# A selective scan on one core: C's rows kept in SBUF, the entering state multiplied in on ScalarE, one more product on GpSimd

## The chip, the core and the metric

The kernel runs on one core of a Trainium2 chip. The metric is device time in microseconds of one execution of the whole program, the median of several runs. Durations of single instructions come from one profiled execution.

## The reference

The input is a float32 image batch of 2 x 96 channels x 128 x 128. Two layers follow each other; each adds a token mixer and then a small quantised feed-forward net. The feed-forward nets and the second layer's mixer (a 3 x 3 convolution) are not touched here. The first layer's mixer is four Mamba scans over the image, in four directions (rows forward, rows backward, columns forward, columns backward), each with 192 inner channels d and 16 states s, over L = 16384 tokens:

```python
def step(h, t):
    dt_t, u_t, B_t, C_t = t
    dA = jnp.exp(dt_t[:, :, None] * A)
    h = dA * h + dt_t[:, :, None] * B_t[:, None, :] * u_t[:, :, None]
    y = jnp.einsum('bds,bs->bd', h, C_t)
    return (h, y)
...
y = ys.transpose(1, 0, 2) + Dp * xc
y = y * jax.nn.silu(z)
return y @ outp_w.T
```

B and C depend on token and state, not on the channel: every one of the 192 channels of a direction is multiplied with the same row. The four results are concatenated and mixed by a 96-row matrix (fuse_w).

## The kernel before

For each of the two images there are three stages: `normalize` (layer norm, and a copy of the image by columns), `mamba` (all scans), and `ffn_and_conv`. The change lies in `mamba` and in the layout of its weights.

**Tiling.** Directions are handled in two pairs (rows forward with columns forward, then the two backward ones). A pair has 2 x 192 = 384 channels, that is NG = 3 groups of 128 partitions: group 0 is the first 128 channels of the first direction, group 2 the last 128 of the second, and the middle group 1 holds 64 channels of each. Tokens are cut in tiles of T = 512. A **step** is one pair and one tile of tokens: 2 x 32 = 64 steps an image. A **unit** is one group and two states: 24 units a step. Two units, so four states, make a **quad**, the piece in which rows of B and C are loaded: [128 partitions, 4 states, 512 tokens], 1 MB.

**Rows of B and C.** For each step a matrix product gives the rows of B and C of both directions (`rows`, L262 to L272), and one DMA writes them to the DRAM tile `bcd` (L277), laid out [B or C, quad of states, direction, state, token]. `row_tile` (L329) loads a quad back, repeated over the partitions. For groups 0 and 2 one direction's rows go to all 128 partitions. For group 1 both directions are needed, and the source is stated as 64 repeats of the pair of directions, so that even partitions get the first direction and odd ones the second:

```python
src = d["bcd"][k, s // 4] if g == 1 else d["bcd"][k, s // 4, g // 2 : g // 2 + 1]
n = src.shape[0]
nc.sync.dma_start(t, src[None].broadcast_to((128 // n, n, 4, T)))
```

So that the channels stand in the same order, the weights of group 1 are permuted on the host (`perm` in `_layout`), and where group 1 comes out of a product in halves, it is written to a tile `mix` first and then moved by two DMAs to even and odd partitions (`mix`, L253 to L256).

**A unit.** GpSimd multiplies a quad of B in place by dt * u (`b_part`, L339). ScalarE writes the two decays exp(dt * A) of a unit into PSUM (`decay`, L349). VectorE scans the two states over 512 tokens (L353); the result goes over the decays in PSUM. VectorE multiplies it by C (L441), into C's tile. TensorE adds the products of all 16 states into one PSUM bank `y` by products with the identity (`sums`, L357). For the six units of `BY_POOL`, (g, s) with s 0 or 8, the scan's result goes to SBUF into B's tile, and GpSimd makes the product with C (L360), since only SBUF is open to it in this kernel. ScalarE keeps each scan's last column in `hst` (L442).

**How a step takes over the state.** Scans start from 0.0. For a step after the first, ScalarE computes the first token's decay for all 16 states of a group (`entry`, L303), GpSimd multiplies it by `hst` (L342) and adds it to the first token of each quad of B (L343).

**Order.** Instructions go to each engine in the order in which the program issues them (`manual_schedule`). The main loop (L469 to L490) runs over units k. At even k it fetches the B quad of unit k + 6 (`B_AHEAD` = 3 quads) and lets GpSimd work on the quad of unit k + 2, then come the scan of the first state, the product and the sums of unit k - 1 (`behind`), the decays of unit k + 2, the scan of the second state, and at even k the fetch of C's quad of unit k + 4 (`C_AHEAD` = 2). `later` puts GpSimd's products one iteration after and their sums three iterations after. The next step's projections, convolutions and activations (`prologue`) are issued between units at fixed places in the previous step. All loads of the stage but two go through SP's queue. `row0` has four buffers and `row1` three; a fetch waits on SP for the sums, products or scans that read the buffer last.

Of the kernel before, what the change touches and what calls it, by code (L numbers as in the profile page):

```python
# [10 lines left out]
F32 = mybir.dt.float32  # L11
# [3 lines left out]
AF = mybir.ActivationFunctionType  # L15
# [16 lines left out]
NG = 3  # L32
B_AHEAD = 3
C_AHEAD = 2
AHEAD = 2
BY_POOL = tuple((g, s) for g in range(3) for s in (0, 8))
BCO = 32
# [4 lines left out]
def tile_metaformer(ctx: ExitStack, tc: tile.TileContext, a: dict, out: bass.AP):  # L42
# [142 lines left out]
    def mamba(acc, xnr, xnc):  # L185

        with ExitStack() as st:
            pool = lambda n, bufs, **kw: st.enter_context(tc.tile_pool(name=n, bufs=bufs, **kw))

            io, gen, one, mixp, two = (pool(*p) for p in (("io", 2), ("gen", 4), ("one", 1), ("mixp", 1), ("two", 2)))  # L190
            ps_w, ps_y, ps_m = (pool(n, k, space=PSUM) for n, k in (("ps_w", 3), ("ps_y", 1), ("ps_m", 1)))
            rows_d = pool("rows_d", 3, space=DRAM)

            hst = one.tile([128, NG, S], F32, name="hst")
            enter = one.tile([128, NG, S], F32, name="enter")
            acc_w = acc.rearrange("c (h w) -> c w h", w=W)
# [17 lines left out]
            def prologue(pi, i, d):  # L214
# [20 lines left out]
                def conv_out(g):  # L235
                    if g == 1:
                        d["xc"] = two.tile([128, NG, T], F32, name="xc")
                    t = mixed("xc") if g == 1 else d["xc"][:, g, :]
                    nc.scalar.activation(t, d["ps"], AF.Identity, bias=convb[:, pi, g : g + 1])  # L239

# [3 lines left out]
                def gate_out(g):  # L244
                    if g == 1:
                        d["sz"] = two.tile([128, NG, T], F32, name="sz")
                    nc.scalar.copy(mixed("sz") if g == 1 else d["sz"][:, g, :], d["ps"])  # L247

                def mixed(name):
                    d["mix", name] = mixp.tile([128, T], F32, name="mix")  # L250
                    return d["mix", name]

                def mix(name):  # L253

                    for k in range(2):
                        nc.sync.dma_start(d[name][k:128:2, 1, :], d["mix", name][64 * k : 64 * k + 64, :])  # L256

# [42 lines left out]

                def entry(g):

                    nc.scalar.activation(enter[:, g, :], amat[:, pi, g, :], AF.Exp, scale=d["dt"][:, g, 0:1])  # L303

                first = pi == 0 and i == 0
                at = [(-3, 1, load), (3, 0, partial(mix, "xc")), (11, 0, partial(silu, "xc"))]
                at += [(9, 0, partial(mix, "sz")), (31, 1, partial(silu, "sz"))]
                at += [(12, 0, rows), (13, 1, rows_out), (14, 0, rows_to_dram)]  # L310
# [9 lines left out]
                for g, k in enumerate((19, 27, 29)):  # L320
                    at += [(k, 0, partial(dt_u, g))]
                    if i > 0:
                        at += [((20, 24, 29)[g], 1, partial(entry, g))]

# [3 lines left out]

            def row_tile(d, g, s, k, ahead):  # L329

                t = gen.tile([128, 4, T], F32, name=f"row{k}", bufs=ahead + 1)

                src = d["bcd"][k, s // 4] if g == 1 else d["bcd"][k, s // 4, g // 2 : g // 2 + 1]
                n = src.shape[0]
                nc.sync.dma_start(t, src[None].broadcast_to((128 // n, n, 4, T)))
                return t

            def b_part(i, d, g, s, b):
                nc.gpsimd.tensor_tensor(b, d["dtu"][g][:, None, :].broadcast_to((128, 4, T)), b, ALU.mult)  # L339
                if i > 0:  # L340
                    if s == 0:
                        nc.gpsimd.tensor_tensor(enter[:, g, :], enter[:, g, :], hst[:, g, :], ALU.mult)  # L342
                    nc.gpsimd.tensor_tensor(b[:, :, 0], b[:, :, 0], enter[:, g, s : s + 4], ALU.add)  # L343

            def decay(pi, d, g, s):

                da = ps_w.tile([128, 2, T], F32, name="da")
                for j in range(2):
                    nc.scalar.activation(da[:, j, :], d["dt"][:, g, :], AF.Exp, scale=amat[:, pi, g, s + j : s + j + 1])  # L349
                return da  # L350

            def scan(j, da, b, h):
                nc.vector.tensor_tensor_scan(h[:, j, :], da[:, j, :], b[:, j, :], 0.0, ALU.mult, ALU.add)  # L353

# [4 lines left out]
            def by_pool(h, c):  # L359
                nc.gpsimd.tensor_tensor(c, h, c, ALU.mult)  # L360

# [52 lines left out]

            def fetch(k, n, ahead, m):
                if k < total:
                    t = row_tile(state[k // nu], *units[k % nu], n, ahead)
                    m[k], m[k + 1] = t[:, 0:2, :], t[:, 2:4, :]
                    if n == 0:
                        quads[k] = t  # L420

            def feed(k):

                if k < total:
                    n = k // nu
                    b_part(steps[n][1], state[n], *units[k % nu], quads.pop(k))

            def feed_decay(k):
                if k < total:
                    n = k // nu  # L430
                    das[k] = decay(steps[n][0], state[n], *units[k % nu])

            ys = {}

            def behind(k):

                n, u = divmod(k, nu)
                (pi, i), d, (g, s) = steps[n], state[n], units[u]
                h, c = hs.pop(k), cs.pop(k)
                if (g, s) not in BY_POOL:  # L440
                    nc.vector.tensor_tensor(c, h, c, ALU.mult)  # L441
                nc.scalar.copy(hst[:, g, s : s + 2], h[:, :, T - 1])  # L442
                if s == 0:
                    if k > 0:
                        pn, pu = divmod(k - 1, nu)
                        gated(steps[pn][0], state[pn], units[pu][0], ys.pop(k - 1))
                    y = ps_y.tile([128, T], F32, name="y")
                    nc.tensor.matmul(y, dmat[:, pi, g, :], d["xc"][:, g, :], start=True, stop=False)  # L448
                else:
                    y = ys.pop(k - 1)  # L450
                ys[k] = y
                if (g, s) in BY_POOL:
                    later(k + 1, 1, True, by_pool, h, c)
                    later(k + 3, 1, True, sums, s, y, c)
                else:
                    sums(s, y, c)
                if k == total - 1:
                    gated(pi, d, g, y)
                if s == S - 2 and g > 0:
                    later(k + 4, 0, True, project, pi, i, d, g)  # L460
                    later(k + 5, 1, False, collect, pi, d, g)

            for m, (n, ahead) in ((bs, (0, B_AHEAD)), (cs, (1, C_AHEAD))):
                for k in range(ahead):
                    fetch(2 * k, n, ahead, m)
            feed(0)
            for k in range(AHEAD):
                feed_decay(k)
            for k in range(total + 6):  # L469
                n, u = divmod(k, nu)  # L470
                if u == nu - 3:

                    prepare(n + 2)
                if k % 2 == 0:
                    fetch(k + 2 * B_AHEAD, 0, B_AHEAD, bs)
                    feed(k + AHEAD)
                issue(k, 0)
                if k < total:
                    (g, s) = units[u]
                    da, b = das.pop(k), bs.pop(k)  # L480
                    hs[k] = b if (g, s) in BY_POOL else da
                    scan(0, da, b, hs[k])
                if 0 < k <= total:
                    behind(k - 1)
                feed_decay(k + AHEAD)
                if k < total:
                    scan(1, da, b, hs[k])
                if k % 2 == 0:
                    fetch(k + 2 * C_AHEAD, 1, C_AHEAD, cs)
                issue(k, 1)  # L490
# [109 lines left out]
def _layout(v):  # L600
# [3 lines left out]

    perm = np.arange(2 * DI)
    perm[128:256] = perm[128:256].reshape(2, 64).T.reshape(-1)
    grouped = lambda w: w.reshape(2, NG, 128, -1).transpose(2, 0, 1, 3)
    plain = lambda w: grouped(w[order].reshape(2, 2 * DI, -1))
    rows = lambda w: grouped(w[order].reshape(2, 2 * DI, -1)[:, perm])
    xw = v["L0_conv_xproj_w"]  # L610
# [12 lines left out]
    for pi, (p, q) in enumerate(PAIRS):  # L623
        ow = v["L0_conv_outp_w"]
        outx[:, pi, 0] = ow[p, :, :128]
        outx[:, pi, 1, 0::2] = ow[p, :, 128:]
        outx[:, pi, 2, 1::2] = ow[q, :, :64]
        outx[:, pi, 3] = ow[q, :, 64:]
# [6 lines left out]
        "convb": plain(v["L0_conv_conv_b"])[..., 0],  # L635
        "bcw": grouped(bcw[:, perm]),
        "dtw": dtw[:, :, perm],
        "dtb": rows(v["L0_conv_dt_b"])[..., 0],
        "alog": rows(v["L0_conv_A_log"]),
        "dskip": rows(v["L0_conv_Dp"])[..., 0],  # L640
        "outx": outx,
# [27 lines left out]
```

## Time and profile before

| What | Value |
|---|---|
| Median of three runs | 11,550.38 us (11,546.19 to 11,551.36) |
| Profiled execution: time | 11,556.77 us |
| Profiled execution: span in the trace | 11,555.0 us |
| Granted TensorE clock, mean | 0.989 |
| HBM read / written | 3289.04 MB / 54.53 MB |
| Packets on SP's DMA queue | 539,960, 3410.16 MB, 76.8% of 16 engines over the span |

The time is that of the whole execution; the span runs from the first to the last recorded instruction. Engines are named PE (TensorE), PEld (its weight loads), DVE (VectorE), ACT (ScalarE), POOL (GpSimd) and SP (SyncE). A row of a group gives line, engine, operation, output and inputs, the count, the busy time, the mean duration of one in ns, and the engine's idle time just before these instructions with what ended it. Idle time of an engine that is not the bound costs nothing by itself.

### The profile page before, as it was taken

Reading aid. Unit: us, or ns where it says so; the run is one execution under the profiler, and the core shown is the slowest. Engines: PE = TensorE matmul, PEld = TensorE weight load, DVE = VectorE, ACT = ScalarE, POOL = GpSimd, SP = SyncE. Lnnn points to the kernel's source line nnn. Section 1 sums busy time; section 2 is a strip of 40 time slices with the busy share of each in tenths; the row PEclk is TensorE's granted clock in tenths of the full one; section 3 lists DMA queues with packets and bytes.
Section 4 is the critical chain, followed back from the end, with each engine's and each line's share of the span. In section 5 each row is a group of like instructions: output and inputs, shape, how many; then the busy total and the mean of one; then the engine's idle time right before and its main releaser. Section 6 shows DMA issues by size and latency. Waiting matters only on the chain. (4 is left out here: it accounts for less than half of the span.)

```text
span 11555.0 us, 94102 instructions
## 1 busy us (share of the span) xinstructions
PE 10435.0 (90%) x24208; PEld 3971.4 (34%) x24208; DVE 10421.6 (90%) x10127; ACT 7901.7 (68%) x13564; POOL 9672.3 (84%) x4700
## 2 busy tenths in 40 slices
PE   7999999999999999989989999999999999999899
PEld 2333333333333333333323333333333333333333
DVE  6999999999999999994469999999999999999944
ACT  6767767677677677665567677677676776776655
POOL 5999999999999999991159999999999999999911
PEclk8999999999999999999989999999999999999999
DMA  7888888888888888880068888888888888888800
GB/s 263 335 329 333 333 332 332 330 331 333 329 332 333 330 331 333 329 322 19 26 243 334 328 331 334 330 333 333 333 331 329 332 332 329 331 333 329 319 13 13
DMA packets 540755, 3416.96 MB, mean 296 GB/s; under 512 B 67532, under 2 KB 68652, under 8 KB 143832
## 3 DMA queue, kind: packets, MB, share of 16 engines
q1 hardware_dynamic: 539960, 3410.16, 76.8%
q8 instruction: 196, 3.21, 0.1%
q14 instruction: 343, 2.81, 0.1%
q0 software_dynamic: 256, 0.79, 0.0%
HBM read 3289.04 MB, written 54.53 MB: 289 GB/s over the span
## 5 line engine op out<-in xcount | busy, mean ns | idle before, releaser
L339 POOL TENSOR_TENSOR row<-dtu,row 128x2048 f32<-128x2048 f32 x1536 | 6948.9, 4524 | 283.3 <-DMA row<-bcd 281.6
L357 PE MATMUL y<-row,ident 128*128 128x512 f32 x12288 | 5690.6, 603 | 700.0 <-DVE row L441 699.9
L353 DVE TENSOR_TENSOR_SCAN da<-da,row 128x512 f32<-128x512 f32 x4608 | 5456.9, 1214 | 38.9 <-ACT da L349 5.2
L349 ACT ACTIVATE da<-dt,amat 128x512 f32<-128x512 f32 x6144 | 4246.9, 691 | 170.2
L357 PEld LDWEIGHTS y<-row,ident 128*128 128x128 f32 x12288 | 2256.8, 190 | 4008.4 <-issue 2243.5
L441 DVE TENSOR_TENSOR row<-da,row 128x1024 f32<-128x1024 f32 x2304 | 2776.7, 1205 | 70.2 <-DMA row<-bcd 70.0
L442 ACT COPY hst<-da 128x2 f32<-128x2 f32 x2304 | 368.9, 160 | 2652.2 <-DVE row L441 2649.3
L360 POOL TENSOR_TENSOR row<-row,row 128x1024 f32<-128x1024 f32 x768 | 1807.4, 2353 | 223.0 <-DVE row L353 147.5
L353 DVE TENSOR_TENSOR_SCAN row<-da,row 128x512 f32<-128x512 f32 x1536 | 1852.4, 1206 | 91.9 <-POOL row L339 84.1
L211 PE MATMUL misc<-xa,inx 96*64 96x512 f32 (+1 forms) x2048 | 946.1, 605 | 50.0 <-ACT mix L239 26.8
L211 PE MATMUL misc<-xb,inx 96*64 96x512 f32 (+1 forms) x2048 | 952.3, 608 | 33.6 <-ACT hst L442 24.2
L564 POOL TENSOR_TENSOR acc<-acc,y 96x512 f32<-96x512 f32 x128 | 147.4, 1151 | 991.5 <-DVE y L563 991.5
L298 POOL TENSOR_TENSOR dtu<-dt,xc 128x512 f32<-128x512 f32 x384 | 487.4, 1269 | 106.0 <-DMA xb<-xnc 99.8
L576 PE MATMUL pc<-pad,kw 96*96 96x512 f32 x1152 | 566.4, 593 | 0.0
L211 PEld LDWEIGHTS misc<-xa,inx 96*64 96x64 f32 (+1 forms) x2048 | 327.3, 165 | 581.2 <-issue 438.0
L448 PE MATMUL y<-xc,dmat 128*128 128x512 f32 x768 | 419.5, 628 | 103.6 <-DVE sz L364 103.6
L374 PE MATMUL misc<-sz,gmat 128*96 128x512 f32 x1024 | 484.1, 595 | 0.0
L284 PE MATMUL misc<-rows,dtw 12*128 12x512 f32 x768 | 434.3, 645 | 50.6 <-ACT dt L289 37.9
L364 DVE TENSOR_TENSOR sz<-y,sz 128x512 f32<-128x512 f32 x384 | 264.6, 689 | 229.5 <-PE y L357 198.0
L136 DVE TENSOR_TENSOR xq<-xm,rs 96x512 fp8e5<-96x512 f32 x128 | 87.9, 687 | 392.2 <-ACT rs L132 392.2
L211 PEld LDWEIGHTS misc<-xb,inx 96*64 96x64 f32 (+1 forms) x2048 | 316.5, 164 | 361.9 <-issue 214.1
L372 PE MATMUL misc<-acc,ident 96*96 96x512 f32 x512 | 387.6, 842 | 57.3 <-ACT sz L247 53.8
(76 smaller groups left out, 7449.9 us busy)
## 6 DMA issues: line engine op xcount, KB each, us to landing
row<-bcd SPq DMA_DIRECT2D x3072, 1024.0 KB, 7.4
xc<-mix SPq DMA_DIRECT2D x256, 128.0 KB, 5.4
sz<-mix SPq DMA_DIRECT2D x256, 128.0 KB, 8.9
xa<-xnr SPq DMA_DIRECT2D x124, 193.1 KB, 8.6
xb<-xnc SPq DMA_DIRECT2D x124, 193.1 KB, 8.7
bcd<-rows SPq DMA_DIRECT2D x128, 128.0 KB, 9.5
acc<-in_x_dram SPq DMA_DIRECT2D x16, 768.0 KB, 5.7
xnr<-xn SPq DMA_DIRECT2D x16, 768.0 KB, 4.3
```

The lines of the kernel that those rows point to most:

```text
L211: nc.tensor.matmul(ps[rows, :], w(PAIRS[pi][d], k, lo, hi), src[d][:, k : k + T], **se)
L284: nc.tensor.matmul(d["ps"], w, d["rows"][0 : 2 * RK, :], start=True, stop=True)
L298: nc.gpsimd.tensor_tensor(dtu, d["dt"][:, g, :], d["xc"][:, g, :], ALU.mult)
L339: nc.gpsimd.tensor_tensor(b, d["dtu"][g][:, None, :].broadcast_to((128, 4, T)), b, ALU.mult)
L349: nc.scalar.activation(da[:, j, :], d["dt"][:, g, :], AF.Exp, scale=amat[:, pi, g, s + j : s + j + 1])
L353: nc.vector.tensor_tensor_scan(h[:, j, :], da[:, j, :], b[:, j, :], 0.0, ALU.mult, ALU.add)
L357: nc.tensor.matmul(y, ident, c[:, j, :], start=False, stop=s + j == S - 1)
L360: nc.gpsimd.tensor_tensor(c, h, c, ALU.mult)
L374: nc.tensor.matmul(d["po"], gmat[:, pi, 2 * g - 2 + k, :], d["yg"][g - 1 + k], start=False, stop=k == 1)
L441: nc.vector.tensor_tensor(c, h, c, ALU.mult)
L448: nc.tensor.matmul(y, dmat[:, pi, g, :], d["xc"][:, g, :], start=True, stop=False)
L576: nc.tensor.matmul(pc, kw[:, t, :], rows, start=t == 0, stop=t == 8)
```

## The change

- C no longer streams. Four tiles `crow` [128, 4, 512], one for each quad of states, are kept. `c_fill` loads all 128 partitions of one for group 0, and then only the half whose direction changes: partitions 64 to 127 for group 1, partitions 0 to 63 for group 2. A fill is issued two quads after the units that read the tile last.
- The product with C is written into B's tile instead of C's.
- B has five buffers and is fetched four quads ahead, after the second scan of an iteration. Its source is now stated as each direction's rows repeated 64 times, one direction after the other, so that group 1 is two halves and not interleaved. `perm`, `mix` and the `mix` tile go.
- The state enters otherwise: ScalarE multiplies the first token's decay in PSUM by `hst`, one column per state, and the scan starts from 1.0 instead of 0.0. `entry`, the tile `enter` and GpSimd's additions go.
- GpSimd makes the products of seven units of 24: s = 2 and 8 of each group, and s = 4 of group 1.
- The scratch memory for DMAs that GpSimd issues is set to 4096 bytes.

```diff
-B_AHEAD = 3
-C_AHEAD = 2
+B_AHEAD = 4
-BY_POOL = tuple((g, s) for g in range(3) for s in (0, 8))
+BY_POOL = tuple((g, s) for g in range(3) for s in (2, 8)) + ((1, 4),)
...
-            def row_tile(d, g, s, k, ahead):
-
-                t = gen.tile([128, 4, T], F32, name=f"row{k}", bufs=ahead + 1)
-
-                src = d["bcd"][k, s // 4] if g == 1 else d["bcd"][k, s // 4, g // 2 : g // 2 + 1]
+            def row_tile(d, g, s):
+
+                t = gen.tile([128, 4, T], F32, name="row", bufs=B_AHEAD + 1)
+                src = d["bcd"][0, s // 4] if g == 1 else d["bcd"][0, s // 4, g // 2 : g // 2 + 1]
                 n = src.shape[0]
-                nc.sync.dma_start(t, src[None].broadcast_to((128 // n, n, 4, T)))
+                nc.sync.dma_start(t, src[:, None].broadcast_to((n, 128 // n, 4, T)))
                 return t
 
+            crow = [one.tile([128, 4, T], F32, name=f"crow{q}") for q in range(S // 4)]
+
+            def c_fill(n, g, q):
+
+                if n < len(steps):
+                    part = (slice(0, 128), slice(64, 128), slice(0, 64))[g]
+                    src = state[n]["bcd"][1, q, int(g > 0)]
+                    nc.sync.dma_start(crow[q][part], src[None].broadcast_to((part.stop - part.start, 4, T)))
+
-            def b_part(i, d, g, s, b):
+            def b_part(d, g, b):
                 nc.gpsimd.tensor_tensor(b, d["dtu"][g][:, None, :].broadcast_to((128, 4, T)), b, ALU.mult)
-                if i > 0:
-                    if s == 0:
-                        nc.gpsimd.tensor_tensor(enter[:, g, :], enter[:, g, :], hst[:, g, :], ALU.mult)
-                    nc.gpsimd.tensor_tensor(b[:, :, 0], b[:, :, 0], enter[:, g, s : s + 4], ALU.add)
...
+                if i > 0:
+                    for j in range(2):
+                        nc.scalar.activation(da[:, j, 0:1], da[:, j, 0:1], AF.Copy, scale=hst[:, g, s + j : s + j + 1])
                 return da
 
-            def scan(j, da, b, h):
-                nc.vector.tensor_tensor_scan(h[:, j, :], da[:, j, :], b[:, j, :], 0.0, ALU.mult, ALU.add)
+            def scan(i, j, da, b, h):
+                nc.vector.tensor_tensor_scan(h[:, j, :], da[:, j, :], b[:, j, :], float(i > 0), ALU.mult, ALU.add)
...
-                h, c = hs.pop(k), cs.pop(k)
+                h, b, c = hs.pop(k), cs.pop(k), crow[s // 4][:, s % 4 : s % 4 + 2, :]
                 if (g, s) not in BY_POOL:
-                    nc.vector.tensor_tensor(c, h, c, ALU.mult)
+                    nc.vector.tensor_tensor(b, h, c, ALU.mult)
...
                 if k % 2 == 0:
-                    fetch(k + 2 * C_AHEAD, 1, C_AHEAD, cs)
+                    fetch(k + 2 * B_AHEAD)
+                    if 4 <= k < total + 4:
+                        cn, cu = divmod(k - 4, nu)
+                        cg, cq = cu // 8, cu % 8 // 2
+                        c_fill(cn + (cg == 2), (cg + 1) % 3, cq)
                 issue(k, 1)
```

More of the change, by code (lines that the diff above doesn't have):

```diff
@@ L188, in mamba @@
             pool = lambda n, bufs, **kw: st.enter_context(tc.tile_pool(name=n, bufs=bufs, **kw))
-            io, gen, one, mixp, two = (pool(*p) for p in (("io", 2), ("gen", 4), ("one", 1), ("mixp", 1), ("two", 2)))
+            io, gen, one, two = (pool(*p) for p in (("io", 2), ("gen", 4), ("one", 1), ("two", 2)))
             ps_w, ps_y, ps_m = (pool(n, k, space=PSUM) for n, k in (("ps_w", 3), ("ps_y", 1), ("ps_m", 1)))
@@ L194, in mamba @@
             hst = one.tile([128, NG, S], F32, name="hst")
-            enter = one.tile([128, NG, S], F32, name="enter")
             acc_w = acc.rearrange("c (h w) -> c w h", w=W)
@@ L237, in conv_out @@
                         d["xc"] = two.tile([128, NG, T], F32, name="xc")
-                    t = mixed("xc") if g == 1 else d["xc"][:, g, :]
-                    nc.scalar.activation(t, d["ps"], AF.Identity, bias=convb[:, pi, g : g + 1])
+                    nc.scalar.activation(d["xc"][:, g, :], d["ps"], AF.Identity, bias=convb[:, pi, g : g + 1])
                 def gate(g):
@@ L246, in gate_out @@
                         d["sz"] = two.tile([128, NG, T], F32, name="sz")
[L247 to L256, printed above, removed]
+                    nc.scalar.copy(d["sz"][:, g, :], d["ps"])
                 def silu(name):
@@ L299, in dt_u @@
                     d["dtu"].append(dtu)
-                def entry(g):
-                    nc.scalar.activation(enter[:, g, :], amat[:, pi, g, :], AF.Exp, scale=d["dt"][:, g, 0:1])
                 first = pi == 0 and i == 0
-                at = [(-3, 1, load), (3, 0, partial(mix, "xc")), (11, 0, partial(silu, "xc"))]
-                at += [(9, 0, partial(mix, "sz")), (31, 1, partial(silu, "sz"))]
+                at = [(-3, 1, load), (11, 0, partial(silu, "xc"))]
+                at += [(31, 1, partial(silu, "sz"))]
                 at += [(12, 0, rows), (13, 1, rows_out), (14, 0, rows_to_dram)]
@@ L321, in prologue @@
                     at += [(k, 0, partial(dt_u, g))]
-                    if i > 0:
-                        at += [((20, 24, 29)[g], 1, partial(entry, g))]
                 outs = (conv_out, gate_out, rows_out, dt_out)
@@ L327, in prologue, with decay @@
                 return sorted(at, key=lambda p: p[:3])
[L329 to L333 removed]
+            def row_tile(d, g, s):
+                t = gen.tile([128, 4, T], F32, name="row", bufs=B_AHEAD + 1)
+                src = d["bcd"][0, s // 4] if g == 1 else d["bcd"][0, s // 4, g // 2 : g // 2 + 1]
                 n = src.shape[0]
[L335 removed]
+                nc.sync.dma_start(t, src[:, None].broadcast_to((n, 128 // n, 4, T)))
                 return t
[L338 to L345 removed]
+            crow = [one.tile([128, 4, T], F32, name=f"crow{q}") for q in range(S // 4)]
[5 more added lines that the diff above has]
+            def b_part(d, g, b):
+                nc.gpsimd.tensor_tensor(b, d["dtu"][g][:, None, :].broadcast_to((128, 4, T)), b, ALU.mult)
+            def decay(pi, i, d, g, s):
                 da = ps_w.tile([128, 2, T], F32, name="da")
@@ L359, in by_pool @@
             def by_pool(h, c):
-                nc.gpsimd.tensor_tensor(c, h, c, ALU.mult)
+                nc.gpsimd.tensor_tensor(h, h, c, ALU.mult)
             def gated(pi, d, g, y):
@@ L413, in mamba, with fetch @@
             bs, cs, das, hs, quads = {}, {}, {}, {}, {}
-            def fetch(k, n, ahead, m):
+            def fetch(k):
                 if k < total:
[L417 to L420, printed above, removed]
+                    quads[k] = t = row_tile(state[k // nu], *units[k % nu])
+                    bs[k], bs[k + 1] = t[:, 0:2, :], t[:, 2:4, :]
             def feed(k):
@@ L425, in feed @@
                     n = k // nu
-                    b_part(steps[n][1], state[n], *units[k % nu], quads.pop(k))
+                    b_part(state[n], units[k % nu][0], quads.pop(k))
             def feed_decay(k):
@@ L430, in feed_decay @@
                     n = k // nu
-                    das[k] = decay(steps[n][0], state[n], *units[k % nu])
+                    das[k] = decay(*steps[n], state[n], *units[k % nu])
             ys = {}
@@ L452, in behind @@
                 if (g, s) in BY_POOL:
-                    later(k + 1, 1, True, by_pool, h, c)
-                    later(k + 3, 1, True, sums, s, y, c)
+                    later(k + 1, 1, True, by_pool, b, c)
+                    later(k + 3, 1, True, sums, s, y, b)
                 else:
-                    sums(s, y, c)
+                    sums(s, y, b)
                 if k == total - 1:
@@ L461, in behind @@
                     later(k + 5, 1, False, collect, pi, d, g)
-            for m, (n, ahead) in ((bs, (0, B_AHEAD)), (cs, (1, C_AHEAD))):
-                for k in range(ahead):
-                    fetch(2 * k, n, ahead, m)
+            for k in range(B_AHEAD):
+                fetch(2 * k)
+                c_fill(0, 0, k)
             feed(0)
@@ L474, in mamba @@
                 if k % 2 == 0:
-                    fetch(k + 2 * B_AHEAD, 0, B_AHEAD, bs)
                     feed(k + AHEAD)
@@ L480, in mamba @@
                     da, b = das.pop(k), bs.pop(k)
+                    cs[k] = b
                     hs[k] = b if (g, s) in BY_POOL else da
-                    scan(0, da, b, hs[k])
+                    scan(steps[n][1], 0, da, b, hs[k])
                 if 0 < k <= total:
@@ L486, in mamba @@
                 if k < total:
-                    scan(1, da, b, hs[k])
+                    scan(steps[n][1], 1, da, b, hs[k])
                 if k % 2 == 0:
-                    fetch(k + 2 * C_AHEAD, 1, C_AHEAD, cs)
+                    fetch(k + 2 * B_AHEAD)
[3 more added lines that the diff above has]
+                        c_fill(cn + (cg == 2), (cg + 1) % 3, cq)
                 issue(k, 1)
@@ L603, in _layout @@
     order = [d for pair in PAIRS for d in pair]
-    perm = np.arange(2 * DI)
-    perm[128:256] = perm[128:256].reshape(2, 64).T.reshape(-1)
     grouped = lambda w: w.reshape(2, NG, 128, -1).transpose(2, 0, 1, 3)
     plain = lambda w: grouped(w[order].reshape(2, 2 * DI, -1))
-    rows = lambda w: grouped(w[order].reshape(2, 2 * DI, -1)[:, perm])
     xw = v["L0_conv_xproj_w"]
@@ L625, in _layout @@
         outx[:, pi, 0] = ow[p, :, :128]
-        outx[:, pi, 1, 0::2] = ow[p, :, 128:]
-        outx[:, pi, 2, 1::2] = ow[q, :, :64]
+        outx[:, pi, 1, :64] = ow[p, :, 128:]
+        outx[:, pi, 2, 64:] = ow[q, :, :64]
         outx[:, pi, 3] = ow[q, :, 64:]
@@ L635, in _layout @@
         "convb": plain(v["L0_conv_conv_b"])[..., 0],
[L636 to L640, printed above, removed]
+        "bcw": grouped(bcw),
+        "dtw": dtw,
+        "dtb": plain(v["L0_conv_dt_b"])[..., 0],
+        "alog": plain(v["L0_conv_A_log"]),
+        "dskip": plain(v["L0_conv_Dp"])[..., 0],
         "outx": outx,
@@ L657 @@
     from concourse.bass_utils import run_bass_kernel_spmd as run
-    nc = bacc.Bacc("TRN2", target_bir_lowering=False, num_devices=1)
+    nc = bacc.Bacc("TRN2", target_bir_lowering=False, num_devices=1, dynamic_dma_scratch_size=4096)
     arrays, args = {}, {}
```

## The prediction

> **What bounds the kernel now.** I read the page's engine shares first, then one window of the scan stage (1000 to 5000 us), then who waits for whom in it, then the DMA queues.
>
> ```profile
> PE 10435.0 (90%) x24208; PEld 3971.4 (34%) x24208; DVE 10421.6 (90%) x10127; ACT 7901.7 (68%) x13564; POOL 9672.3 (84%) x4700
> ```
>
> Three engines lie near 90%, so the shares alone decide nothing. In the window (columns: length, then busy time of PE, PEld, DVE, ACT, POOL, clock, DMA share, GB/s):
>
> ```profile
> 1000.00:5000.00 4000.00, 3643.30 (x8395) 1385.63 (x8394) 3868.18 (x3487) 2819.86 (x4843) 3758.18 (x1807) 1.00 0.86 332
> ```
>
> DVE is busy 96.7%. Its groups there (count, then busy us and mean ns):
>
> ```profile
> L353 DVE TENSOR_TENSOR_SCAN da<-da,row 128x512 f32<-128x512 f32 x1819 | 2153.6, 1214 | 12.5
> L353 DVE TENSOR_TENSOR_SCAN row<-da,row 128x512 f32<-128x512 f32 x606 | 730.8, 1206 | 2.8 <-POOL row L343 2.6
> L441 DVE TENSOR_TENSOR row<-da,row 128x1024 f32<-128x1024 f32 x910 | 1096.6, 1205 | 26.6 <-DMA row<-bcd 26.5
> L339 POOL TENSOR_TENSOR row<-dtu,row 128x2048 f32<-128x2048 f32 x607 | 2746.6, 4525 | 111.5 <-DMA row<-bcd 110.4 <-ACT da L349 0.3
> L360 POOL TENSOR_TENSOR row<-row,row 128x1024 f32<-128x1024 f32 x303 | 713.1, 2354 | 83.8 <-DVE row L353 54.6 <-issue 27.9 <-DMA row<-bcd 0.3
> L343 POOL TENSOR_TENSOR row<-row,enter 128x4 f32<-128x4 f32 x594 | 119.1, 201 | 46.6
> L442 ACT COPY hst<-da 128x2 f32<-128x2 f32 x909 | 145.6, 160 | 1035.8 <-DVE row L441 1034.7
> ```
>
> A step has 24 units and 48 scans; 1819 + 606 = 2425 scans in 4000 us are 50.5 steps, so a step takes **79.2 us** and a unit 3.3. Per step DVE works 0.967 x 79.2 = 76.6, POOL 0.940 x 79.2 = 74.4, ACT 55.8. There are 64 steps for each of two images: 128 x 79.2 = 10,138 us; the other 1,417 of the span (11,555.0) are stages that the change does not touch. The row loads are late only a little (26.5 us before DVE and 110.4 before POOL in 4000). DVE is the bound, and the DMA is close behind:
>
> ```profile
> q1 hardware_dynamic: 51556, 331.28, 85.5%
> row<-bcd SPq DMA_DIRECT2D x304, 1024.0 KB, 7.3
> ```
>
> These are of 3000 to 4000 us: packets, MB, busy share of 16 engines; then issues, size, us to landing. An engine moves 331.28 MB / (0.855 x 16 x 1000 us) = 24.2 KB per us, so an 8192-byte packet costs 0.338 us on average. In the trace's packet records its median is 0.311 and its lowest 0.307.
>
> **The change, part by part.**
>
> *One DVE product fewer (7 of 24 to POOL instead of 6).* DVE loses 1.2 us a step: 75.4. POOL gains 2.35 and loses the 12 additions at 0.20 and three entry products at 0.22: 74.4 + 2.35 - 2.4 - 0.7 = 73.7. The order DVE over POOL stays. The other stalls of DVE (2.6 us a step, mostly before the gating product) stay, but for 0.5 on C's loads: a step of about 77.7.
>
> *The state enters on ScalarE.* 48 copies of one column a step. The nearest row is the two-column copy, 0.160; the wider entry activation takes 0.294. So 7.7 to 14.1 us, less three entry activations (0.9): ACT reaches 62.6 to 69.0 of 77.7. ACT waited 1034.7 / 50.5 = 20.5 us a step for DVE before the state copy: that idle time hides them, and the decays run two units ahead of their scans. I take 0; without that cover it would be 7.7 us a step.
>
> *The interleave goes.* Four SBUF copies of 128 KB a step leave SP's queue. Nothing on the path waited for them: 0.
>
> *C stays in SBUF.* A step loads 12 quads of B (1 MB each) and refills C with four full and eight half quads (8 MB): 20 MB instead of 24. A refill is issued on SP behind B's fetch. At worst that fetch waits for the sums of a GpSimd unit, at the end of iteration k+2, and the refilled rows are read in iteration k+5: 2.5 units, 8.1 us, against 7.3 to land today, with less traffic. I take 0; late fills are a rival below. The B tile now holds the product too, so its buffer comes free a product later than today; four quads ahead instead of three pay for that.
>
> *B's middle group.* This decides. For g = 1 both directions' rows are needed. Before, the source was stated as 64 pairs of rows (outer count 64, then 2). After the change it is 2 rows, each 64 times (outer count 2). How a transfer is dealt to the engines is visible in the landing marks on its semaphore: transfers with 128, 96 or 64 outer rows leave 16 marks; the one transfer here with 12 outer rows, the load of dtw (L51), leaves 12 together and a single one about 13 us ahead of them. So a transfer with outer count 12 ran on 12 engines. No row has an outer count of 2. Bounds: 16 engines, as the 64 x 2 form has it (8 packets each, 2.5 us), or **2 engines**, if the outer count limits it as it did for dtw: 64 packets each. I take 2, by the dtw row, and the same two each time.
>
> [...] No run shown here has the case of 2.
>
> Price: 64 x 0.311 = 19.9 us a quad on both engines, four a step. These four are fetched while group 0 is worked on, and I take it that what SP sends later waits behind them on these two engines (no row shows one transfer overtaking another). From the first middle fetch (end of iteration 0) the order on them is: quad 4; C's fill for group 0, q 2 (8 packets, 2.5 us); quad 5; fill q 3 (2.5); quad 6; half fill (4 packets, 1.25); quad 7; half fill (1.25). Sum 4 x 19.9 + 7.5 = 87.1, and about 2 to land (2.1 is the shortest median among the page's landings). GpSimd's product of unit 10 and DVE's of unit 11 need the last fill: DVE stands there until 89. From iteration 12 to 24, 12.5 units at 3.24 = 40.5, to the next step's first middle fetch, which waits for the sums before it (about 3, five matmuls of 0.6). The step is 89 + 41 + 3 = **133 us**, and 128 x 133 + 1,417 = **18,440 us**. This stands on the profiled execution's 11,555 span (11,557 whole), 6 us above the median shown, which is nothing here.
>
> Bounds within this case. Low: the two engines never idle. Per step 4 x 64 + 8 x 8 + 4 x 8 + 8 x 4 = 384 packets x 0.311 = 119.4, and 2 for the small transfers: 121.4, so 16,960. High: packets at 0.338 (+7) and 7 more a step for SP held by a late buffer and a TensorE whose clock falls while it idles (0.90 in the first 300 us, PE 79% busy): 147, so 20,230.
>
> **The rivals.**
>
> *A: the middle loads spread over 16 engines.* Then the one DVE product counts: 79.2 to 77.7, 128 x 1.45 = 186 less, **11,370** (11,300 to 11,500). For it: the same 1 MB in 128 descriptors of 8 KB lands in 7.3 us today. Against it: the 12 marks. It decides where a quad takes less than its share of two units, 6.5 us: 128 x 0.311 / 6.5 = 6.1 engines, so 8 suffice; 4 would give 256 packets a step, 80 us, about no change. Chance 0.13.
>
> *B: two engines, but other ones each time.* The four middle quads then run side by side, 19.9 plus some 7 of queue and landing, against 6 units (19.4 us) from fetch to need: 8 us late once a step, 128 x 6.5 net = 830 more, **12,400**. For it: nothing; no row shows it. Chance 0.04.
>
> *C: 16 engines, but refills come late behind SP's waits.* The longest landing in 1000 to 5000 us is 12.5 against a lead of 8.1: 4.4 us late at most, three times a step, less the 1.45 gained: up to 11.7 x 128 = 1,500 more; a third of it is likelier, **11,900**. The gap to SP's idle time speaks against it:
>
> ```profile
> SPq L335 <- PE y L357: 2719.1, 555, 10.0
> ```
>
> SP waits for buffers (2719 of 4000 us) rather than for the queue, and traffic falls by a sixth. Chance 0.03.
>
> **How the numbers follow.** The two-engine case has 0.80 and predicts 18,440; its bounds, 16,950 to 20,250, are the range, since the rest is 0.20. About 0.2% (23 us) is what a measurement can tell from no change. Faster: A less a sliver, 0.12. Same: 0.02 (four engines, or C and A in balance). Slower: 0.86.
>
> **What would show it.** Right: middle B loads land in 20 to 80 us and the median of the edge ones stays under 10 where nothing is queued; GB/s falls to 20 MB / 133 us = about 155; DVE's share in the stage falls to 75.4 / 133 = 57%, with its idle time before the product and the scan put down to the row transfers; landing marks fall to 2 or 3 for 512 transfers. The column copies last 0.16 to 0.29 and nobody waits for them. Wrong: a DMA mean near 260 GB/s with DVE at 97% would be A; one short stall a step, B; waits on the crow tiles alone, C.

## The result and the profile after

The changed kernel takes **21,718 us** in the median (21,707 to 21,732) against 11,551: ratio 1.880, 95% interval 1.877 to 1.884. I had forecast slower, 18,440, and a range up to 20,250; the time lies above it. By the prediction's own division a step takes (21,718 - 1,417) / 128 = 158.6 us instead of 79.2; all steps below are worked out in this way.

The engines' shares on the page of the changed kernel:

```profile
PE 12397.1 (57%) x24208; PEld 4642.2 (21%) x24208; DVE 10395.1 (48%) x9999; ACT 8972.4 (41%) x19144; POOL 9608.1 (44%) x2968
```

No engine is near its limit; DVE's and GpSimd's busy time is what it was, spread over nearly twice the time. The chain that ended last says what took their place:

```profile
DMA 55%; PE 28%; DVE 4%; ACT 4%; issue 4%; POOL 3%; SPq 1%; another core or an unknown queue 0%; DVEq 0%; POOLq 0%; ACTq 0%
DMA crow<-bcd 53%; PE y L344 17%; DVE row L426 3%; DMA row<-bcd 3%; PE pc L565 2%; PE misc L209 2%; PE misc L361 2%; POOL row L327 2%; POOL row L347 2%; PE misc L359 1%; ACT da L333 1%; SPq L314 1%; PE v L127 1%; PE xm L121 1%; PE y L433 1%
```

Stretches of the changed kernel (columns as in the prediction): the stage, 18 us of one step in which a middle quad is loaded, and 12 us of the same step later on:

```profile
1000.00:5000.00 4000.00, 2213.11 (x4160) 827.23 (x4159) 1913.79 (x1704) 1618.99 (x3538) 1850.82 (x552) 0.74 0.41 135
3012.00:3030.00 18.00, 4.80 (x8) 1.38 (x8) 3.48 (x3) 2.54 (x6) 6.81 (x2) 0.59 0.13 53
3094.00:3106.00 12.00, 8.43 (x15) 2.91 (x14) 7.69 (x8) 5.47 (x14) 11.50 (x4) 0.86 0.91 273
```

The second row is the reading of this case: a DMA share of 0.13 is two engines of sixteen (2/16 = 0.125), they move 53 GB/s, and DVE works 3.5 of 18 us. In the third row nearly all engines move data again (0.91, 273 GB/s) and GpSimd is busy for 11.5 of 12 us. The DMA view of the same 18 us:

```profile
DMA packets 116, 0.95 MB, mean 53 GB/s; under 512 B 0, under 2 KB 0, under 8 KB 0
...
q1 hardware_dynamic: 116, 0.95, 12.6%
```

116 packets on two engines in 18 us are 0.310 us each. Four waits of DVE in this step, one behind each slow quad (start, length, instruction; idle time before it and what ended it):

```profile
3012.05 1.23 DVE L426 TENSOR_TENSOR row<-da,crow 128x1024 f32<-128x1024 f32 x1 [14.02 <-DMA crow<-bcd]
3035.81 1.22 DVE L426 TENSOR_TENSOR row<-da,crow 128x1024 f32<-128x1024 f32 x1 [20.28 <-DMA crow<-bcd]
3060.67 1.22 DVE L426 TENSOR_TENSOR row<-da,crow 128x1024 f32<-128x1024 f32 x1 [18.03 <-DMA crow<-bcd]
3085.15 1.22 DVE L426 TENSOR_TENSOR row<-da,crow 128x1024 f32<-128x1024 f32 x1 [15.80 <-DMA crow<-bcd]
```

From the packet records of 1000 to 5000 us, the share of time in which so many DMA engines were busy at once:

```
busy engines     0      1     2-3    4-12   13 or more
before        10.2%   2.1%   1.0%    3.8%   82.9%
after         11.9%   2.9%  50.0%    3.1%   32.1%
```

Half of the time two or three engines are busy: 0.500 x 158.6 = 79.3 us a step, against 4 x 19.9 = 79.6 forecast. In the step above SP issues the four middle loads 0, 13, 25 and 60 us after the first, and the first one's last marks come 26 and 27 us after its issue (3008.7 and 3009.5): so two wait at once. Yet 4 to 12 engines are busy only 3.1% of the time, so they use the same two: rival B is out. The landing marks agree: 66,029 before (16 for each of 4,127 transfers, but 13 for `dtw`) and 51,181 after. The change removes the four `mix` copies of each step, 512 transfers of 16 marks each (8,192 marks); a step still has 12 loads of B, and 12 fills of C in place of 12 loads. The middle load that SP issues at 2982.64 leaves 3 marks instead of 16: a single one at 2983.6, then two at 3008.7 and 3009.5, as `dtw` left a single one and then 12. With 3 for each of the 512 middle loads (6,656 fewer) the sum is 66,029 - 8,192 - 6,656 = 51,181, to the unit.

Who waits, in the same window of the changed kernel (engine, line, what for; us in total, times, longest):

```profile
DVE row L426 <- DMA crow<-bcd: 1948.8, 172, 21.4
...
POOL row L327 <- DMA row<-bcd: 897.1, 103, 22.0
POOL row L347 <- DMA crow<-bcd: 887.3, 51, 19.8
```

DVE waits for C's fills. They are short where no slow load is ahead of them (the one issued at 2981.48 has all 16 marks by 2988.7, after 7.2 us), but queue behind the slow quads: the one issued at 2996.48, just after the middle load of 2995.90, has 14 marks by 3012.0 and the other two at 3034.8 and 3035.7, after that load's last two at 3031.2 and 3033.1. DVE's product starts at 3035.81. By the prediction's own sign, waits on the crow tiles alone would speak for rival C; e2, which has no such tiles, decides between the two. The groups that answer to those of before (1000 to 5000 us, count, busy us and mean ns, idle before):

```profile
L340 DVE TENSOR_TENSOR_SCAN da<-da,row 128x512 f32<-128x512 f32 x852 | 1012.6, 1215 | 58.7 <-POOL row L327 53.5
...
L426 DVE TENSOR_TENSOR row<-da,crow 128x1024 f32<-128x1024 f32 x426 | 516.5, 1212 | 1949.7 <-DMA crow<-bcd 1948.8 <-DVE da L340 0.4
L340 DVE TENSOR_TENSOR_SCAN row<-da,row 128x512 f32<-128x512 f32 x351 | 418.6, 1204 | 0.0
L347 POOL TENSOR_TENSOR row<-row,crow 128x1024 f32<-128x1024 f32 x176 | 413.3, 2348 | 1255.0 <-DMA crow<-bcd 887.3 <-ACT hst L427 367.5
```

The durations are those of before (1215, 1212, 1204, 2348 ns): these instructions of DVE and GpSimd run no slower, there is only waiting. The last row shows a second releaser, ScalarE's state copy L427, that was not there before; e4 takes it up.

### The profile page after: what moved, and what is told of

Read it like the earlier page. It is cut to its first block, busy times and chain, and to the rows that moved or that the text cites. A ratio compares the mean times of both kernels' runs of the same rounds, so it can differ in the third digit from the quotient of the medians.

```text
span 21718.9 us, 95160 instructions
## 1 busy us (share of the span) xinstructions
PE 12397.1 (57%) x24208; PEld 4642.2 (21%) x24208; DVE 10395.1 (48%) x9999; ACT 8972.4 (41%) x19144; POOL 9608.1 (44%) x2968
## 4 chain that ended last, share of the span: by engine, by line
DMA 55%; PE 28%; DVE 4%; ACT 4%; issue 4%; POOL 3%; SPq 1%; another core or an unknown queue 0%; DVEq 0%; POOLq 0%; ACTq 0%
DMA crow<-bcd 53%; PE y L344 17%; DVE row L426 3%; DMA row<-bcd 3%; PE pc L565 2%; PE misc L209 2%; PE misc L361 2%; POOL row L327 2%; POOL row L347 2%; PE misc L359 1%; ACT da L333 1%; SPq L314 1%; PE v L127 1%; PE xm L121 1%; PE y L433 1%
## 5 line engine op out<-in xcount | busy, mean ns | idle before, releaser
L344 PE MATMUL y<-row,ident 128*128 128x512 f32 x12288 | 7130.2, 732 | 6455.3 <-DVE row L426 6302.0
L426 DVE TENSOR_TENSOR row<-da,crow 128x1024 f32<-128x1024 f32 x2176 | 2638.4, 1212 | 9857.6 <-DMA crow<-bcd 9855.0
L340 DVE TENSOR_TENSOR_SCAN da<-da,row 128x512 f32<-128x512 f32 x4352 | 5172.8, 1215 | 375.4 <-POOL row L327 340.2
L344 PEld LDWEIGHTS y<-row,ident 128*128 128x128 f32 x12288 | 2832.6, 238 | 10725.3 <-issue 7628.9
L347 POOL TENSOR_TENSOR row<-row,crow 128x1024 f32<-128x1024 f32 x896 | 2104.4, 2349 | 6268.3 <-DMA crow<-bcd 4441.8
L427 ACT COPY hst<-da 128x2 f32<-128x2 f32 x2176 | 351.3, 161 | 10824.0 <-DVE row L426 10823.9
L340 DVE TENSOR_TENSOR_SCAN row<-da,row 128x512 f32<-128x512 f32 x1792 | 2136.8, 1204 | 0.0
L433 PE MATMUL y<-xc,dmat 128*128 128x512 f32 x768 | 553.7, 810 | 1926.0 <-DVE sz L351 1926.0
L336 ACT ACTIVATE da<-da,hst 128x1 f32<-128x1 f32 x5952 | 1149.8, 232 | 96.4
L209 PE MATMUL misc<-xa,inx 96*64 96x512 f32 (+1 forms) x2048 | 940.0, 601 | 28.1 <-DMA xa<-xnr 17.4
L254 PE MATMUL misc<-xc,bcw 128*96 128x512 f32 x768 | 608.1, 956 | 407.4 <-ACT xc L247 407.4
L433 PEld LDWEIGHTS y<-xc,dmat 128*128 128x128 f32 x768 | 140.3, 229 | 2242.4 <-DVE sz L351 2139.8
L286 POOL TENSOR_TENSOR dtu<-dt,xc 128x512 f32<-128x512 f32 x384 | 485.4, 1264 | 75.6 <-DMA xb<-xnc 33.8
```

The source lines that it names most:

```text
L209: nc.tensor.matmul(ps[rows, :], w(PAIRS[pi][d], k, lo, hi), src[d][:, k : k + T], **se)
L336: nc.scalar.activation(da[:, j, 0:1], da[:, j, 0:1], AF.Copy, scale=hst[:, g, s + j : s + j + 1])
L344: nc.tensor.matmul(y, ident, c[:, j, :], start=False, stop=s + j == S - 1)
L347: nc.gpsimd.tensor_tensor(h, h, c, ALU.mult)
L426: nc.vector.tensor_tensor(b, h, c, ALU.mult)
```

## The experiments

Theory: the middle loads on two engines make the time. First rival: C's single resident copy, refilled in halves behind SP's waits, makes it.

**e1: the middle quads of B in two halves.**

```diff
-nc.sync.dma_start(t, src[:, None].broadcast_to((n, 128 // n, 4, T)))
+for j in range(n):
+    part = slice(j * 128 // n, (j + 1) * 128 // n)
+    nc.sync.dma_start(t[part], src[j : j + 1].broadcast_to((128 // n, 4, T)))
```

> The changed kernel with each middle quad of B loaded by two transfers of 64 outer rows (partitions 0 to 63, then 64 to 127) in place of one with outer count 2; all else is kept. Two-engine theory: the four loads a step spread over 16 engines again, the 2-engine stretches vanish, the step falls from 158.6 to 78 to 83 us: 11,400 to 12,000. Rival, C's single resident copy with its half refills behind SP's waits costs the time: it is all still there, so the time stays above 16,000.

Measured: 13,777 us, ratio to before 1.193 (1.191 to 1.195), step 96.6; two or three engines are busy 1.1% of the stage (1000 to 5000 us):

```profile
1000.00:5000.00 4000.00, 3274.55 (x6840) 1252.90 (x6838) 3146.72 (x2799) 2640.03 (x5755) 3043.98 (x909) 0.90 0.76 222
```

So the form of the load is worth 62.0 us a step of the 79.4 lost. But 13,777 is far above the 12,000 of my theory: without any slow load the changed kernel still loses 17.4 us a step against the kernel before.

**e2: the same form put into the kernel before.**

```diff
+outer = src[:, None].broadcast_to((n, 128 // n, 4, T)) if k == 0 else src[None].broadcast_to((128 // n, n, 4, T))
-nc.sync.dma_start(t, src[None].broadcast_to((128 // n, n, 4, T)))
+nc.sync.dma_start(t, outer)
```

> The kernel before with one line changed: the middle quads of B (not of C) are loaded with outer count 2. The rows of B then reach the wrong half of group 1's channels, so the output is not the reference's; the amount of work is the same. Two-engine theory: four quads of 19.9 us a step on the same two engines, with four quads of C (2.5 us each) between them, then some 14 units at 3.3 until the next one is fetched: 90 + 46 = 136 us or more a step, 18,000 to 22,000. Rival, refills of a resident C cost the time: there is none here, 11,550.

Measured (one run): 21,145 us, step 154.1, with 50.0% of the stage on two or three engines and 59,373 landing marks (66,029 - 512 x 13). DVE's waits in 1000 to 5000 us, the first one through GpSimd's work on the quad of B, the second for C's quads behind it:

```profile
DVE da L354 <- POOL row L344: 1035.3, 52, 24.6
DVE row L442 <- DMA row<-bcd: 810.4, 52, 17.7
```

They are 71 us a step. The one line by itself adds 154.1 - 79.2 = 74.9 us a step and nearly doubles the time; nothing else of the change is needed. It is also 18 us above the 136 that the sum of the expectation gives.

**e3: C's fills ahead of B's fetches** (after the change `fetch` came first).

```diff
 if k % 2 == 0:
-    fetch(k + 2 * B_AHEAD)
     if 4 <= k < total + 4:
...
         c_fill(cn + (cg == 2), (cg + 1) % 3, cq)
+    fetch(k + 2 * B_AHEAD)
```

> The changed kernel with each fill of C issued ahead of B's fetch of the same iteration, so that it no longer waits behind that fetch for a buffer of B; the middle loads stay on outer count 2. Theory that the recovery stretch is late because of SP's order: DVE's waits for crow after the middle loads (4.3 + 5.4 us and about 1.5 smaller in the step looked at) go, and the step falls by 8 to 15 us: 19,800 to 20,700. Rival, the two engines alone set the step: 21,700, unchanged within 1%.

Measured: 21,031 us, ratio 1.823 (1.819 to 1.826), step 153.2: 5.4 us less, below the 8 to 15 expected, but not the rival's 0. SP's order costs something beside the two engines. DVE's waits of 1000 to 5000 us show why it is not more:

```profile
DVE row L426 <- DMA crow<-bcd: 807.7, 52, 17.4
DVE da L340 <- POOL row L327: 628.1, 28, 25.1
DVE row L340 <- POOL row L327: 497.3, 50, 20.3
```

The waits for C fall from 1948.8 to 807.7 us, but waits for the slow quads of B themselves, through GpSimd's product, grow from 53.5 to 1125.4.

**e4: the whole change on the row order of before** (interleaved rows, `perm` and `mix` back; half fills on every second partition; the scratch memory of GpSimd's DMAs is 2048 bytes here, in e5 to e7 and in e11).

```diff
-part = (slice(0, 128), slice(64, 128), slice(0, 64))[g]
+part = (slice(0, 128), slice(1, 128, 2), slice(0, 128, 2))[g]
-nc.sync.dma_start(t, src[:, None].broadcast_to((n, 128 // n, 4, T)))
+nc.sync.dma_start(t, src[None].broadcast_to((128 // n, n, 4, T)))
```

> The changed kernel with the row order of the kernel before: middle quads of B as 64 x 2, weights permuted, the tile mix and its four copies a step back; C's half fills go to odd and even partitions instead of the upper and lower half. Two-engine theory: no transfer of outer count below 64 is left; DVE binds with one product fewer, step 77.7 to 79: 11,360 to 11,530. Rival, late refills: above 12,000, with DVE waiting on crow.

Measured: 13,124 us, ratio 1.137 (1.135 to 1.138), step 91.5. No slow form is left, and it is still 13.7% slower than before. The waits of e4 in 1000 to 5000 us:

```profile
ACT hst L437 <- DVE row L436: 853.6, 481, 5.3
POOL row L357 <- ACT hst L437: 746.3, 215, 5.9
DVE row L436 <- DMA crow<-bcd: 323.6, 129, 5.0
```

Two waits that the kernel before does not have. DVE's product waits for late fills, 7.4 us a step. And GpSimd's product waits for ScalarE, 17.1 us a step: it is now made in place, over the scan's result, and ScalarE must first have copied the last state from there. GpSimd's busy 73.8 and this wait are 91 of 91.5.

**e5, e6, e7: each of these two taken away, then both**, on e4. e5 and e7 have the order of e3; e6 and e7 let GpSimd copy the states of its own units:

```diff
 def by_pool(h, c, g, s):
+    nc.gpsimd.tensor_copy(hst[:, g, s : s + 2], h[:, :, T - 1])
     nc.gpsimd.tensor_tensor(h, h, c, ALU.mult)
...
-nc.scalar.copy(hst[:, g, s : s + 2], h[:, :, T - 1])
+if (g, s) not in BY_POOL:
+    nc.scalar.copy(hst[:, g, s : s + 2], h[:, :, T - 1])
```

> The interleaved kernel (13,124, step 91.5 us) with each fill of C issued ahead of B's fetch. Theory of late fills: DVE's 7.5 us a step of waiting for crow go and what follows from them, step 84 or less: under 12,200. Theory of the in-place GpSimd product (it overwrites the scan's result in B's tile, so it has to wait until ScalarE has copied the last state from there; GpSimd waits 17.2 us a step for that copy, 73.8 busy + 17.2 = 91.0): GpSimd sets the step, time within 2% of 13,124, and the waits for crow vanish or move.

> The interleaved kernel with the last state of GpSimd's seven units copied by GpSimd itself, just ahead of its product, in place of ScalarE; the order of fills and fetches as in the change. Theory of the in-place product: GpSimd's 17.2 us a step of waiting go, 7 copies of 0.2 us come: step 78 to 84, 11,400 to 12,200. Theory of late fills: unchanged, 12,900 to 13,200, with DVE still waiting for crow 5 us a step or more.

> The interleaved kernel with both edits: fills ahead of fetches and GpSimd copying its own states. Both theories together: no wait of the three is left, DVE binds with one product fewer than the kernel before: step 77.7 to 79, 11,360 to 11,530. If it stays above 11,800, a third cause is at work.

Measured: e5 12,290 (ratio 1.064, 1.062 to 1.065; step 84.9), e6 13,039 (1.127, 1.125 to 1.130; 90.8), e7 11,893 (1.030, 1.028 to 1.031; 81.8). The late fills are the larger loss, 6.6 us, though e5 stays a little above its 12,200. GpSimd's wait costs 0.7 while fills are late and 3.1 once they are not. In e4 it was mostly time in which GpSimd would have waited anyway: in e6 it waits 15 us a step for DVE, for loads and for ScalarE's decays instead. The addition to 91 misled. e7 misses its 11,530: a third cause.

**e8: both edits on the changed kernel, slow form kept.**

> The changed kernel, middle loads still on outer count 2, with both edits. If the two engines alone made the 133 us a step that I predicted and the two waits made the rest of 158.6, it is back near 133: 17,000 to 19,500. If the two-engine stretches hold the step up by themselves, since four quads of 19.9 us and what queues behind them cannot be overlapped, it stays above 20,300.

Measured: 21,081 (1.825, 1.822 to 1.827), step 153.6, no better than e3. Beside the slow loads GpSimd's wait is worth nothing, and with both edits the step is still over 20 us above my 133.

**e9, e10, e11: the other parts alone in the kernel before**: ScalarE entry with seven GpSimd products, ScalarE entry with six, and the resident C with both mendings (as e7, but with `enter` and six products).

> The kernel before (C streamed, interleaved) with two parts of the change alone: the state enters on ScalarE, and GpSimd makes seven products, (g, s) with s 0 or 8 and (1, 4). Theory that the ScalarE entry is the third cause (in e7 DVE idles 6.1 us a step against 2.6 in the kernel before, 1.7 of it for the column copies, and ScalarE holds its queue 7.2 us a step for TensorE): 75.4 of work and about 6 of waiting, step 81 to 82, 11,780 to 11,920. Rival, the resident C or the in-place product costs it: step 77.7, 11,330 to 11,420, faster than both kernels.

> The kernel before with the ScalarE entry alone, six products on GpSimd as before. Entry theory: DVE's work stays 76.6 and its waits grow by 3 us a step: 11,850 to 12,050. Rival: the copies are hidden by ScalarE's idle time, as I predicted: 11,480 to 11,570.

> The kernel before with the resident C alone: interleaved rows, half fills to odd and even partitions issued ahead of fetches, the product in B's tile, GpSimd copying the states of its own six units, and the state entering through enter and GpSimd as before. Entry theory: DVE's waits are those of the kernel before, step 79 to 80, 11,500 to 11,650. Rival: the resident C costs it, step near e7's 81.9 plus one product: 11,850 to 12,050.

Measured: e9 11,918 (1.032, 1.031 to 1.034; step 82.0), e10 11,989 (1.038, 1.036 to 1.039; 82.6), e11 11,991 (1.039, 1.037 to 1.040; 82.6). So both parts make the kernel slower by themselves: the ScalarE entry by 3.4 us a step, the resident C by 3.4 even when mended (against the entry theory's 11,650). The seventh GpSimd product, measured on top of the entry (e10 to e9), gains 0.6 us, half of the 1.2 expected. ScalarE's copies in e10 (1000 to 5000 us):

```profile
L339 ACT ACTIVATE da<-da,hst 128x1 f32<-128x1 f32 x2280 | 440.4, 232 | 36.9
```

and DVE's two groups that wait there:

```profile
L343 DVE TENSOR_TENSOR_SCAN da<-da,row 128x512 f32<-128x512 f32 x1745 | 2070.0, 1215 | 67.8 <-ACT da L339 47.1 <-ACT hst L432 14.7 <-POOL row L350 0.6
...
L354 DVE TENSOR_TENSOR sz<-y,sz 128x512 f32<-128x512 f32 x145 | 99.9, 689 | 179.7 <-PE y L347 165.8 <-ACT hst L432 13.9
```

A step has 47 copies of 0.23, 9.1 us (48, but none in the first step of a scan). ScalarE's wait for DVE before the state copy shrinks from 20.5 to 13.1 us a step, so idle time takes up most of them. But ScalarE reaches its other instructions later: TensorE's waits for ScalarE (PE and PEld rows together) grow from 398 to 650 us in the 4000, and DVE's wait for y before the gating product from 1.5 to 3.4 us a step. In e11 it is GpSimd and TensorE that are late (waits in the same window):

```profile
POOL hst L365 <- DVE row L358: 255.4, 190, 3.3
DVE sz L370 <- PE y L362: 225.3, 97, 5.8
PEld y L362 <- POOL row L348: 191.8, 124, 2.3
```

**e12: e8 with half fills on every second partition.**

> e8 with one more edit: C's half fills go to odd or even partitions, while the weights stay in halves, so the rows of C meet the wrong channels in groups 1 and 2 and the output is not the reference's; the amount of work is the same. In e8 a fifth of the 8 KB packets take 0.55 to 0.80 us, twice the median; the fills of 64 neighbouring partitions are suspected. If the two engines are busy nearly all the time and the slow packets lie on their chain, 8 half fills x 4 packets x 0.31 us go: step 153.5 to about 143, 19,600 to 20,100. If these bursts are hidden, 21,080 within 1%.

Measured: 20,462 (1.773, 1.770 to 1.775), step 148.8: 4.8 less, half of what was expected, and more than the rival's 0. The packets of 0.55 to 0.80 us fall from 20.1% of the 8 KB ones to 9.7%, so many packets to 64 neighbouring partitions do take twice the median of 0.31 us. Where B's middle quads are halved too the same holds: 33.8% of the packets are that long in e1 and 2.9% in e4. Why they take longer no run shows.

**e13, e14: one and two slow quads a step** (the rest as in e1).

> The changed kernel with only the first of the four middle quads of a step on outer count 2, the other three as two half loads of 64 outer rows. Additive theory: transfers on two engines and on 16 do not overlap, so each slow quad costs its 19.9 us less the two half loads in its place (8 packets of about 0.63 = 5): 14.9 us, 13,777 + 128 x 14.9 = 15,700. Rival, a single slow quad is covered by its lead (fetched 8 units ahead, needed after 6, 19 us) and the loss comes from four in a row: below 14,500.

> The same with the first two middle quads of a step on outer count 2. Additive theory: 13,777 + 2 x 1,910 = 17,600, on the straight line to the changed kernel's 21,718 with four. Rival: the second one is the first that is not covered, 15,500 to 16,500.

Measured: e13 16,370 (1.418, 1.416 to 1.420), e14 18,044 (1.563, 1.560 to 1.565). With none, one, two and four slow quads the step is 96.6, 116.8, 129.9 and 158.6: 20.2 for the first, 13.1 for the second, 14.3 for each of the last two, 15.5 on average against the additive theory's 14.9. The first one costs the most, so the four-quad lead does not cover it; e13 lies above the additive theory's 15,700 and e14 above its 17,600.

## Why the prediction was wrong

- **Two engines, the same two, 19.9 us a quad:** right, by the marks, the stretches of two busy engines (79.3 us a step) and e2. That the four loads of a step would take the same two was an assumption: no run shown before the result has an outer count of 2. In the changed kernel two such loads are outstanding at once, and 4 to 12 engines are busy for only 3.1% of the time.
- **The step that failed** is the sum "89 + 41 + 3": 89 us until DVE's wait behind the last slow quad ends, then 12.5 units at full speed and a wait of 3. From the traces, mean of 24 steps each (us a step), from the issue of the first middle quad to that of the next step; the slow stretch ends with DVE's last wait of over 8 us:

```
                              after     e3     e8    e12     e2   forecast
slow stretch                  101.7  113.8  113.5  108.2  111.0   89
  2 or 3 DMA engines busy      78.5   72.5   71.8   73.0   71.6   79.6
  13 or more busy              19.7   36.2   36.4   31.1   35.1    7.5
rest of the step               57.6   40.5   40.1   39.8   43.1   44
```

The slow quads took what was forecast for them in the changed kernel. The term of 7.5 for what else runs on their two engines was too small: it measured 19.7. It counts four fills, 384 packets of 8 KB; 806 were moved. Left out are the loads still under way when the first slow quad is issued (nearly all engines are busy for the first 8 us of the step from 2983, a DMA share of 0.93), the first quad of group 2 and a third half fill, and many packets of half fills take double (0.55 to 0.80 us, e12). The rest of the step took 57.6 for 44: 13.5 of it are waits of DVE, 9.2 of these for C's fills, for which "C stays in SBUF ... I take 0" left nothing. The two misses, 12.7 and 13.6, are the 26 us above 133.
- **They trade against each other.** With fills ahead of fetches (e3, e8, e12) the rest of the step is 40 us, as forecast, but the slow stretch grows to 108 to 114, because more of the step's other loads run inside it: 1226 packets in e3. e2, with no resident C and no ScalarE entry, has 111.0 and 43.1. So the slow stretch was forecast too short also without the other parts; no run with four slow quads came near 133. What four of them add, forecast 133 - 77.7 = 55.3 us, measured 62.0 against e1 and 74.9 in e2.
- **The zeros for the other parts** were wrong as well: without slow loads I had 77.7, and e1 has 96.6. The runs without slow loads divide these 18.9: half loads and half fills on neighbouring partitions 5.1 (e1 to e4, with the row order, its copies and the scratch memory), fills behind B's fetch 6.6 (e4 to e5), the in-place GpSimd product 3.1 (e5 to e7), and 4.1 that are left in e7. Of these last the entry alone could be all (e9: 4.3 above 77.7), but the resident C alone loses 3.4 too (e11), so the parts do not add. Nor do they add to the slow loads: mending the second of them there gained 5.4 (e3), the second and third 5.0 (e8), and half fills on every second partition 4.8 more (e12).
- **Rival C**, late refills, came on top of the slow loads; I gave it 0.03 and only as an alternative. Its reason against, that SP idles 2719 of 4000 us, was misread: SP idles in a wait for a buffer, and what stands behind that wait in program order is late all the same (6.6 us a step, e4 to e5).
- **The ScalarE entry:** the price of the copies was inside its bounds (9.1 in 7.7 to 14.1). What failed is "idle time hides them": the idle time stands in one place of ScalarE's program, before the state copy, and the copies in another, right behind the decays. The idle time shrank, and 3.4 us a step were lost all the same (e10); and DVE's scans did wait for the copies, 47.1 us in the 4000.
- **One product fewer:** DVE's work fell to 75.9 us a step as forecast, 75.4. It was worth 0.6 us where DVE still nearly binds (e10 to e9); in the changed kernel no run separates it. Its sum was slightly off: 75.4 + 2.6 - 0.5 gives 77.5, not 77.7; and the shortest landing before is 1.8 us (the load of `ident`), not 2.1. Neither matters here.
- **The in-place product** I missed: I priced B's longer-held buffer, not that GpSimd now overwrites what ScalarE has yet to read.
- Not settled: how the 3.4 us of e11 divide, why the second slow quad costs less than the others, and whether TensorE's clock (0.74 in the stage, 0.59 beside a slow load) has a part in DVE's waits for y, 2.2 us in the rest of a step.

## What to carry to other kernels

Before a load is rewritten, look at the outermost count of its source: here a count of 2 put 1 MB on two engines of sixteen and cost 15 to 19 us each (e1, e2), with most of the bandwidth idle (53 GB/s beside such a load, 332 in the stage before). When such loads share a queue with others, count every transfer that runs between them, and not only those that the chain waits for. Ask where in its program an engine's idle time stands before added work is put down as hidden: here ScalarE waited 20.5 us a step in another place than the 9.1 us of copies, and with three engines near 90% the new waits reached the bound (3.4 us a step, e10). Test parts alone: three of the four here lost time by themselves (e2, e10, e11).

## What the runs showed of the hardware

SP's issue of a transfer mostly lasts about 0.5 us, but 9 to 25 us in the rows below, where slow loads are outstanding, and SP issues the next one only after it. What holds it there no view shows. SP in the changed kernel, by time (start, length, line, transfer):

```profile
3156.25 0.53 SPq L314 DMA_DIRECT2D row<-bcd  x1
3156.83 10.14 SPq L324 DMA_DIRECT2D crow<-bcd  x1
3167.08 0.51 SPq L314 DMA_DIRECT2D row<-bcd  x1
3167.63 24.65 SPq L324 DMA_DIRECT2D crow<-bcd  x1
3203.38 0.51 SPq L314 DMA_DIRECT2D row<-bcd  x1
3203.93 8.98 SPq L324 DMA_DIRECT2D crow<-bcd  x1
```

ScalarE's product of one column in PSUM takes 0.232 us, more than its copy of two columns to SBUF (0.162; both in e10).
